# A graph layer on one core: three of five node blocks summed by weight matrices instead of two, blocks of 125 nodes

## The chip, the cores and the metric

One core of a Trainium2 chip. The metric is the device time of one execution in microseconds. The engines are named as in the profile: PE is TensorE, DVE is VectorE, ACT is ScalarE, POOL is GpSimd, SP is SyncE, which issues most DMAs.

## The reference

625 nodes with 512 features, 20,625 edges sorted by destination (20,000 random ones and one loop per node), four edge types with a weight matrix and a bias row each. Cut to what matters:

```python
h = relu(layernorm(x))
msg[e] = (h[src[e]] @ W_rel[type[e]] + b_rel[type[e]]) * weight[e]
agg = segment_sum(msg, dst) / maximum(segment_sum(weight, dst), 1)
z = h @ W_self + b_self + agg
x1 = layernorm(h + z) * ln1_g + ln1_b
ffn = gelu(x1 @ W_ffn1 + b_ffn1) @ W_ffn2 + b_ffn2
out = x + layernorm(x1 + ffn) * ln2_g + ln2_b
```

## The kernel before

Nodes lie in five blocks of 128 rows; 625 nodes leave a gap of 15 rows at the end of block 1. The work has two stages.

**The table stage.** For each relation r and block i, `table_rows` (L350) multiplies the transposed h of the block by W_rel[r] on PE (four matmuls of 512 columns into one PSUM bank). VectorE scales the rows by the norm's factor and adds b_rel, which lies in SBUF spread over all partitions (`brel_bc`), in one instruction (L362). SP stores the 128 rows to a table in DRAM (L365). The tiles m turn over three buffers; the last five of the 20 (`KEPT`) also stay in SBUF. Beside this loop, written out by hand in program order (L798 to L846), VectorE and GpSimd find for every node the window of 64 edge slots in which its edges lie (`find_tiles`, `find_windows`, gathers at L446), and edge indices become table rows (`edge_columns`).

**How an outer block is summed.** For the two blocks 0 and 4 (`dense`) the sum over edges is a matrix product: a weight matrix `sums_w` (table row by destination node, 20 chunks of 128 by 128) is multiplied by the whole table, 20 matmuls per block (`chunk_sum`, L1007). The weight matrix itself is built from the slots in four units per block. A unit is `slot_hots` on VectorE (five instructions: one-hot rows `low`, `eq`, three products `high`), then four banks of `slot_sums` on PE (L602), each emptied by a reduction on VectorE (L608). Before units begin, `turn_fields` transposes slot fields on PE. Five of the eight units are done in the table stage (`EARLY`), at most two banks behind a table row (`PER_ROW`). Table chunks that aren't kept are loaded two at a time (`chunk_load`, L1002, three buffers).

**How an inner block is summed.** For blocks 1 to 3, GpSimd gathers one table row per edge and partition, 128 edges to a gather (L887), after each fourth a pause of two small memsets (L883). Three gathers form a group, whose edges of one partition mostly share a destination: ScalarE scales the first (L893), VectorE adds the other two (L911), and PE multiplies the sum by a one-hot matrix of destinations (L930). Every second group is split into a high and a low part first (L897, L901), and then multiplied in two faster matmuls (L927, L928). There are 33 groups; rows whose group doesn't share a destination come in by six gathers of first rows (L937).

**The second stage** besides holds the self part (L375, L379), the first norm of each block, its transposition (L313, L1049), and the feed-forward part up (L685), Gelu (L689), down (L703), the second norm, the store (L754). Here the order on each engine comes from a planner (`Plan`, L69): each operation has an engine, an assumed duration, buffers, predecessors and a rank. It lists them in assumed time, and the resulting order is fixed in the program: an engine stops at an instruction whose input isn't there. The feed-forward parts follow the order 0, 4, 1, 2, 3 of blocks. If a check at run time finds edges outside the planned windows, a slow path at the end computes everything anew; it isn't taken here.

The loads are issued on SP in program order: x, W_rel of two relations, b_rel and the six bias and norm rows spread over 128 partitions early; others after each relation (`later_loads`, L227).

Of the kernel before, what the change touches and what calls it, by code (L numbers as in the profile page):

```python
# [16 lines left out]
P = 128  # L17
# [4 lines left out]
class EdgePlan:  # L22
# [3 lines left out]
    def __init__(self, n_nodes, n_tiles, n_free, nb):  # L26
# [15 lines left out]
        self.gap = nb * P - n_nodes  # L42
        self.gap_at = 2 * P - self.gap
        self.first = [b * P - (self.gap if b > 1 else 0) for b in range(nb)]
        self.size = [P - (self.gap if b == 1 else 0) for b in range(nb)]
# [19 lines left out]
    def row(self, node):  # L65
        return node + (self.gap if node >= self.gap_at else 0)
# [70 lines left out]
def gnn_layer(ctx, tc, x, edges, edge_groups, firsts, fourths, windows, w_self, w_rel, w_ffn1, w_ffn2, rows_in, bf1_in, out, n_edges):  # L137
# [22 lines left out]
    ep = EdgePlan(N, NT, n_edges - N, NB)  # L160
    NC = R * NB
# [24 lines left out]
    brel_bc = early.tile([P, R * D], F32, name="brel_bc")  # L186
# [7 lines left out]
    def load_x(b0, b1):  # L194
        nc.sync.dma_start(xs[:, b0:b1, :], x[ep.first[b0]:ep.first[b0] + (b1 - b0) * P, :].rearrange("(b p) d -> p b d", p=P))
# [24 lines left out]
    load_rows(brel_bc[:, :D], 0, D)  # L220
# [3 lines left out]
    load_rows(brel_bc[:, D:], D, R * D)  # L224
    load_rows(rows, R * D, (R + 6) * D)

    def later_loads(r):  # L227
        if r == 0:
            load_wr(2)
            nc.sync.dma_start(ws_sb, w_self.rearrange("(k p) n -> p k n", p=P))  # L230
            nc.sync.dma_start(bf1, bf1_in)
        if r == 1:
            load_wr(3)
            nc.sync.dma_start(w1_sb, w_ffn1.rearrange("(k p) f -> p k f", p=P))
        if r == 2:
            nc.sync.dma_start(w2_sb, w_ffn2.rearrange("(k p) n -> p k n", p=P))
# [17 lines left out]
    x_step = const.tile([P, INNER, EG], F32, name="x_step")  # L254
# [17 lines left out]
    grid = mid.tile([P, P, TB], BF16, name="grid")  # L272
    keys = mid.tile([P, 2 * NC, TP], BF16, name="keys")
    ident_b = mid.tile([P, P], BF16, name="ident_b")

    def node_constants():
# [11 lines left out]
        nc.gpsimd.iota(grid, pattern=[[1, P], [0, TB]], base=0, channel_multiplier=0,  # L288
                       allow_small_or_imprecise_dtypes=True)

    def aggregate(st, name, scaled=False):
        mv = work.tile([P, 2], F32, tag="mv", name=f"mv_{name}", bufs=HOTS)
        nc.vector.bn_aggr(mv, st)
        t = work.tile([P, 3], F32, tag="rs", name=f"rs_{name}", bufs=HOTS)
        if scaled:
            nc.vector.tensor_scalar(t[:, 0:1], mv[:, 1:2], EPS, RS ** -2, op0=ALU.add, op1=ALU.mult)
        else:
            nc.vector.tensor_scalar(t[:, 0:1], mv[:, 1:2], EPS, None, op0=ALU.add)
        return mv[:, 0:1], t
# [47 lines left out]
    KEPT = 5  # L347
    kept = {}

    def table_rows(r, i, between=None):  # L350
# [11 lines left out]
        nc.vector.scalar_tensor_tensor(m, p, rx[:, i, 1:2], brel_bc[:, r * D:(r + 1) * D],  # L362
                                       op0=ALU.mult, op1=ALU.add)
        row0 = r * NP + i * P
        nc.sync.dma_start(table[row0:row0 + P, :], m)  # L365
# [21 lines left out]
    node_of = early.tile([P, NT], I32, name="node_of")  # L387
# [14 lines left out]

    def edge_columns():
        nc.vector.tensor_copy(fl, ed[:, 0:3, :])
        nc.vector.tensor_scalar(shift, fl[:, 0:2, :], float(ep.gap_at), float(ep.gap), op0=ALU.is_ge, op1=ALU.mult)
        nc.vector.tensor_add(fl[:, 0:2, :], fl[:, 0:2, :], shift)
        nc.vector.scalar_tensor_tensor(row_i, typ_f, float(NP), src_f, op0=ALU.mult, op1=ALU.add)
        nc.vector.tensor_copy(node_of, dst_f)
        nc.vector.tensor_scalar(node_of, node_of, P - 1, None, op0=ALU.bitwise_and)
        nc.vector.tensor_copy(dst_mod, node_of)  # L410
# [60 lines left out]
    slots = early.tile([P, 3, ND, SL], I32, name="slots")  # L471
    fields = mid.tile([P, ND, 5, 2, SL], BF16, name="fields")
# [19 lines left out]
    def slot_fields():  # L492
        row, low, high = (slots[:, q] for q in range(3))
        src_, typ_, step, high_ = (slot_f[:, q] for q in range(4))
# [4 lines left out]
        nc.vector.tensor_scalar(step, src_, float(ep.gap_at), float(ep.gap), op0=ALU.is_ge, op1=ALU.mult)  # L499
        nc.vector.tensor_add(src_, src_, step)  # L500
        nc.vector.tensor_copy(row, src_)
        nc.vector.tensor_scalar(low, row, P - 1, None, op0=ALU.bitwise_and)
        nc.vector.tensor_scalar(high, row, 7, None, op0=ALU.logical_shift_right)
        nc.vector.tensor_copy(fields[:, :, 0], both(low))
        nc.vector.tensor_copy(high_, high)
        nc.vector.scalar_tensor_tensor(fields[:, :, 1, 0], typ_, float(NB), high_, op0=ALU.mult, op1=ALU.add)
# [6 lines left out]

    def first_edges():
        before_node(before[:, 2, :], ends_w[:, :, 0:4], 4)
        nc.vector.scalar_tensor_tensor(before[:, 2, :], at_f[:, 1, :], 4.0, before[:, 2, :], op0=ALU.mult, op1=ALU.add)
        near = 1.5 * 2.0 ** 23
        g = xw[:, 1, :]
        nc.vector.tensor_scalar(g, before[:, 2, ND:], -(GROUP0 * P + (EG - 1) / 2), 1.0 / EG, op0=ALU.add, op1=ALU.mult)
        nc.vector.tensor_scalar(g, g, near, None, op0=ALU.add)  # L520
        nc.vector.tensor_scalar(g, g, -near, 0.0, op0=ALU.add, op1=ALU.max)
# [8 lines left out]
    def first_columns():  # L530

        nc.vector.tensor_copy(x_cols, x_edges[:, :, :, 0:3])
        for f in range(2):
            nc.vector.tensor_scalar(x_step, x_cols[:, :, :, f], float(ep.gap_at), float(ep.gap), op0=ALU.is_ge, op1=ALU.mult)
            nc.vector.tensor_add(x_cols[:, :, :, f], x_cols[:, :, :, f], x_step)
# [38 lines left out]
    def slot_hots(d, u):  # L574
# [4 lines left out]
        low = mid.tile([P, nb_, P, TB], BF16, tag="low", name=f"low_{d}_{u}", bufs=2)  # L579
# [6 lines left out]
        nc.vector.tensor_tensor(low, of[:, 0].rearrange("p (a t) -> p a t", t=TB).unsqueeze(2).to_broadcast([P, nb_, P, TB]),  # L586
                                grid.unsqueeze(1).to_broadcast([P, nb_, P, TB]), op=ALU.is_equal)
# [6 lines left out]
    def slot_sums(d, u, q, low, high, place):  # L594
        if (d, u, q) == (d, 0, 0):
            sums_w[OUTER[d]] = const.tile([P, NC, P], F32, name=f"sums_w{d}")
# [3 lines left out]
        for i in range(QT):  # L600
            t = q * QT + i
            nc.tensor.matmul(p[:, i * W:(i + 1) * W], low[:, t // TB, :, t % TB], high[:, t // TP, :, t % TP],  # L602
# [3 lines left out]
    def empty_sums(d, u, q, p):  # L606
        n0 = 2 * (u * UNIT + q * QT)
        nc.vector.tensor_reduce(  # L608
            sums_w[OUTER[d]][:, :, n0:n0 + 2 * QT].rearrange("p c (t h) -> p t h c", h=2),
            p[:, :QT * 3 * 2 * NC].rearrange("p (t a h c) -> p t h c a", t=QT, a=3, h=2),  # L610
# [64 lines left out]
    def feed_forward(x1T_b, box, members, name, halves=False):  # L675
# [15 lines left out]
        def down(i):  # L691
# [14 lines left out]
            def summed(h):  # L706
                c = cols[h]
                if h == 0:
                    got["y"] = edge.tile([P, D], F32, tag="ow", name=f"y_{name}_{i}", bufs=OW)
                    got["st"] = work.tile([P, 2, 6], F32, tag="bn", name=f"st_y{name}_{i}", bufs=HOTS)  # L710
                    if n < P:
                        nc.vector.tensor_copy(got["y"], zi)
                nc.vector.tensor_add(got["y"][:n, c], po[h][:n, :c.stop - c.start], zi[:n, c])  # L713

            def stats_(h):
                nc.vector.bn_stats(got["st"][:, h, :], got["y"][:, cols[h]])

            def mean_():
                got["mean"], got["t"] = aggregate(got["st"][:, :len(cols), :], f"y{name}_{i}")

            def centred():
                got["a"] = edge.tile([P, D], F32, tag="ow", name=f"ya_{name}_{i}", bufs=OW)
                nc.vector.scalar_tensor_tensor(got["a"], got["y"], got["mean"], g2_bc,
                                               op0=ALU.subtract, op1=ALU.mult)

            def scaled():
                for c in (slice(0, 5 * D // 8), slice(5 * D // 8, D)) if halves else cols:
                    nc.vector.scalar_tensor_tensor(got["y"][:, c], got["a"][:, c], got["t"][:, 1:2], xi[:, c],
# [7 lines left out]
            for h in range(len(cols)):  # L736
                w = (cols[h].stop - cols[h].start) / D
                norm.append((f"y{h}", "DVE", 0.66 * w + (0.5 if n < P else 0.0), lambda h=h: summed(h),
# [37 lines left out]
    EARLY = 5  # L776
    PER_ROW = 2
    with tc.manual_schedule(engines={PE, DVE, ACT, mybir.EngineType.Pool}):
# [460 lines left out]
```

## Time and profile before

| What | us |
|---|---|
| Median of three runs (lowest, highest) | 285.38 (283.54, 285.41) |
| The profiled execution | 286.26 |
| Its span, first to last instruction | 284.5 |
| PE busy in the span | 248.5 |
| DVE busy | 198.4 |
| ACT busy | 51.5 |
| POOL busy | 139.9 |

The page's busy times are per engine; PEld, the load of weights into PE, overlaps PE. A float matmul appears as two records, so 80 products appear as x160. In a group of instructions the figures behind the bar are busy time, the mean of one in ns, and the idle time of the engine just before them with what ended it. In the timeline a matmul's start is when it begins to stream and its end is modelled, so durations of neighbours overlap; the distance of starts is the pace. In the table by stage, a count stands behind each busy time, then the TensorE clock that was granted (1.00 is full), the busy share of the DMA engines and the rate.

### The profile page before, as it was taken

Reading aid. Unit: us, or ns where it says so; the run is one execution under the profiler, and the core shown is the slowest. Engines: PE = TensorE matmul, PEld = TensorE weight load, DVE = VectorE, ACT = ScalarE, POOL = GpSimd, SP = SyncE. Lnnn points to the kernel's source line nnn. Section 1 sums busy time; section 2 is a strip of 40 time slices with the busy share of each in tenths; the row PEclk is TensorE's granted clock in tenths of the full one; section 3 lists DMA queues with packets and bytes.
Section 4 is the critical chain, followed back from the end, with each engine's and each line's share of the span. In section 5 each row is a group of like instructions: output and inputs, shape, how many; then the busy total and the mean of one; then the engine's idle time right before and its main releaser. Section 6 shows DMA issues by size and latency. Waiting matters only on the chain.

```text
span 284.5 us, 3070 instructions
## 1 busy us (share of the span) xinstructions
PE 248.5 (87%) x952; PEld 138.4 (49%) x952; DVE 198.4 (70%) x451; ACT 51.5 (18%) x104; POOL 139.9 (49%) x196
## 2 busy tenths in 40 slices
PE   7989949999999899999887999738999999744991
PEld 2534414555544454454345745316849576313970
DVE  5561777897697997967694499785567888494014
ACT  3100000000100020211022422202505342200330
POOL 6153610000500477777777777777777777711000
PEclk9999998999999999999998999975999999975797
DMA  7999992511112978898887666766656676721001
GB/s 248 333 415 393 382 352 106 184 74 74 42 50 97 318 210 295 253 317 312 292 325 234 185 187 215 209 199 183 189 154 186 183 208 192 217 75 38 0 2 39
DMA packets 22693, 56.69 MB, mean 199 GB/s; under 512 B 3057, under 2 KB 3777, under 8 KB 22546
## 3 DMA queue, kind: packets, MB, share of 16 engines
q0 software_dynamic: 8896, 28.29, 33.3%
q1 hardware_dynamic: 13632, 28.05, 27.2%
q8 instruction: 8, 0.13, 0.2%
q10 hardware_dynamic: 146, 0.13, 0.1%
q14 instruction: 11, 0.09, 0.1%
HBM read 49.93 MB, written 6.52 MB: 198 GB/s over the span
## 4 chain that ended last, share of the span: by engine, by line
PE 26%; DMA 21%; DVE 19%; POOL 16%; issue 13%; ACT 2%; SPq 1%; POOLq 0%; ACTq 0%; DVEq 0%
DMA ms<-table,row_i 15%; PE pt L355 10%; POOL ms L887 10%; PE pu L685 8%; PE po L703 4%; DVE ea L911 3%; DMA xs<-in_x_dram 3%; DMA win<-in_windows_dram,at_i 2%; PE acc L930 2%; POOL dst L446 2%; DVE es L911 2%; DVE sums_w L608 1%; POOL zeros L883 1%; DVE z L942 1%; ACT ea L893 1%
## 5 line engine op out<-in xcount | busy, mean ns | idle before, releaser
L887 POOL DMA_INDIRECT ms<-table,row_i x99 | 99.3, 1003 | 51.0 <-issue 24.2
L355 PE MATMUL pt<-wr,hT 128*128 128x512 f32 x160 | 73.6, 608 | 0.0
L685 PEld LDWEIGHTS pu<-x1T,w_sb 128*128 128x128 f32 x320 | 43.2, 216 | 7.7 <-issue 4.2
L911 DVE SCALAR_TENSOR_TENSOR ea<-ms,wgt_g,ea 128x512 f32<-128x512 f32 x43 | 32.3, 750 | 19.3 <-ACT ea L893 11.0
L355 PEld LDWEIGHTS pt<-wr,hT 128*128 128x128 f32 x160 | 29.8, 195 | 31.9 <-issue 31.0
L685 PE MATMUL pu<-x1T,w_sb 128*128 128x128 f32 (+1 forms) x320 | 43.4, 299 | 2.0 <-ACT x1T L1049 2.0
L893 ACT ACTIVATE ea<-ms,ed 128x512 f32<-128x512 f32 x33 | 22.8, 691 | 114.8 <-DMA ms<-table,row_i 70.8
L930 PE MATMUL acc<-es,oh 128*128 128x512 f32 x46 | 27.0, 671 | 14.8 <-DVE es L911 14.8
L703 PE MATMUL po<-w_sb,gT 128*128 128x512 f32 (+3 forms) x96 | 36.4, 522 | 0.0
L1007 PE MATMUL acc<-tr,sums_w 128*128 128x512 f32 x60 | 29.0, 598 | 0.0
L703 PEld LDWEIGHTS po<-w_sb,gT 128*128 128x128 f32 (+1 forms) x96 | 16.5, 188 | 14.0 <-issue 11.4
L911 DVE SCALAR_TENSOR_TENSOR es<-ms,wgt_g,ea 128x512 f32<-128x512 f32 x23 | 17.1, 744 | 8.0 <-DMA ms<-table,row_i 7.9
L362 DVE SCALAR_TENSOR_TENSOR m<-pt,rx,brel_bc 128x512 f32<-128x512 f32 x20 | 15.0, 748 | 10.0 <-PE pt L355 8.2
L526 POOL DMA_INDIRECT x_edges<-in_edge_groups_dram,x_group x3 | 2.8, 947 | 37.1 <-DVE x_group L522 36.5
L608 DVE TENSOR_REDUCE sums_w<-bank 128x160 f32<-128x480 f32 x32 | 20.0, 651 | 0.0
L930 PEld LDWEIGHTS acc<-es,oh 128*128 128x128 f32 x46 | 7.9, 200 | 24.3 <-DVE es L911 22.1
L375 PE MATMUL pz<-ws_sb,hT 128*128 128x512 f32 x40 | 18.6, 597 | 0.0
L602 PEld LDWEIGHTS <-low 128*128 128x128 bf16 x128 | 11.5, 147 | 13.2 <-issue 11.2
L689 ACT ACTIVATE gT<-pu,bf 128x128 f32<-128x128 f32 (+1 forms) x40 | 13.7, 362 | 21.1 <-PE pu L685 20.9
L1007 PEld LDWEIGHTS acc<-tr,sums_w 128*128 128x128 f32 x60 | 10.9, 190 | 9.8 <-issue 9.1
L713 DVE TENSOR_TENSOR y<-po,z 128x512 f32<-128x512 f32 (+3 forms) x6 | 3.6, 598 | 17.1 <-PE po L703 17.0
L883 POOL MEMSET zeros<- 128x200 bf16 x48 | 13.2, 274 | 1.4
(160 smaller groups left out, 235.9 us busy)
## 6 DMA issues: line engine op xcount, KB each, us to landing
tr<-table SPq DMA_DIRECT2D x14, 512.0 KB, 5.5
table<-m SPq DMA_DIRECT2D x20, 256.0 KB, 2.3
w_sb<-in_L_gnn_W_ffn_dram SPq DMA_DIRECT2D x2, 2048.0 KB, 10.8
wr<-in_L_gnn_W_rel_dram SPq DMA_DIRECT2D x3, 1024.0 KB, 9.0
ms<-table,row_i POOLq DMA_INDIRECT x99, 3.8
rows<-in_rows_dram SPq DMA_DIRECT2D x1, 1536.0 KB, 13.3
ws_sb<-in_L_gnn_W_self_dram SPq DMA_DIRECT2D x1, 1024.0 KB, 10.6
brel_bc<-in_rows_dram SPq DMA_DIRECT2D x1, 768.0 KB, 10.9
```

Source lines behind the costliest of these rows:

```text
L355: nc.tensor.matmul(p, hT[i][:, k, :], wr_sb[r][:, k, :], start=(k == 0), stop=(k == KD - 1))
L362: nc.vector.scalar_tensor_tensor(m, p, rx[:, i, 1:2], brel_bc[:, r * D:(r + 1) * D], op0=ALU.mult, op1=ALU.add)
L375: nc.tensor.matmul(p[0], hT[i][:, k, :], ws_sb[:, k, :], start=(k == 0), stop=(k == KD - 1))
L608: nc.vector.tensor_reduce(sums_w[OUTER[d]][:, :, n0:n0 + 2 * QT].rearrange("p c (t h) -> p t h c", h=2), p[:, :QT * 3 * 2 * NC].rearrange( ...
L685: nc.tensor.matmul(pu[:, :nn], w1_sb[:, k, f * P:(f + 1) * P], x1T_b()[:, k, :nn], start=(k == 0), stop=(k == KD - 1))
L703: nc.tensor.matmul(po[h][:n, :w], box["gT"][:, f, at], w2_sb[:, f, c], start=(f == 0), stop=(f == KF - 1))
L883: nc.gpsimd.memset(zeros[:, :PAUSE], 0.0)
L887: nc.gpsimd.indirect_dma_start(out=ms[j], out_offset=None, in_=table[:, :], in_offset=bass.IndirectOffsetOnAxis(ap=row_i[:, j:j + 1], axis=0))
L893: nc.scalar.activation(box["sum"], ms[j], AF.Copy, scale=wgt[:, j:j + 1])
L911: nc.vector.scalar_tensor_tensor(to, ms[j], wgt_g[:, k, q - 1:q], box["sum"], op0=ALU.mult, op1=ALU.add)
L930: nc.tensor.matmul(acc[bs], ohs[0][:, q, :].bitcast(F32), box["sum"], start=(k == 0), stop=last)
L1007: nc.tensor.matmul(acc[b,], sums_w[b][:, c, :], kept[(b, c) if (b, c) in kept else c], start=first, stop=last)
```

## The change

Blocks have 125 nodes each, in tiles of 128 rows (`NG = 125`). Blocks 0, 1, 2 are summed by weight matrices, blocks 3 and 4 by gathers. Row 125 of each chunk of the table holds b_rel of its relation, and row 125 of each weight matrix holds sums of the edge weights (a column of ones in `low`), so that b_rel comes in with the chunk sums. For the gathered blocks it comes in by one matmul of degrees by relation (`deg_T`) and b_rel. Table rows are evicted by ScalarE, 125 of them, without a bias, and stored from 125 partitions. `sums_w` has two buffers for three blocks: the units of block 2 come after the chunk sums of block 0. Seven of twelve units are early, at most three banks behind a table row; nine chunks are kept. Loads of bias rows, W_self and the feed-forward weights are issued later. The feed-forward order is 0, 1, 3, 2, 4. Some planner levels are changed. The core of the diff:

```diff
-        self.dense = (0, nb - 1)
+        self.dense = tuple(range(nb - 2))
...
+        self.each = -(-n_nodes // nb)
+        self.first = [b * self.each for b in range(nb)]
...
     def row(self, node):
-        return node + (self.gap if node >= self.gap_at else 0)
+        return node // self.each * P + node % self.each
...
-    load_rows(brel_bc[:, :D], 0, D)
...
-    load_rows(brel_bc[:, D:], D, R * D)
-    load_rows(rows, R * D, (R + 6) * D)
+    nc.sync.dma_start(brel, brel_in[:, :D])
...
         if r == 0:
             load_wr(2)
-            nc.sync.dma_start(ws_sb, w_self.rearrange("(k p) n -> p k n", p=P))
-            nc.sync.dma_start(bf1, bf1_in)
+            bias_rows()
         if r == 1:
             load_wr(3)
+            nc.sync.dma_start(ws_sb, w_self.rearrange("(k p) n -> p k n", p=P))
+            load_rows(rows, 0, 6 * D)
+            nc.sync.dma_start(bf1, bf1_in)
+        if r == 2:
             nc.sync.dma_start(w1_sb, w_ffn1.rearrange("(k p) f -> p k f", p=P))
-        if r == 2:
             nc.sync.dma_start(w2_sb, w_ffn2.rearrange("(k p) n -> p k n", p=P))
...
-    KEPT = 5
+    KEPT = 9
...
+    def bias_rows():
+        n = (P - NG) * D
+        nc.sync.dma_start(bass.AP(tensor=table.tensor, offset=table.offset + NG * D, ap=[[NP * D, R], [P * D, NB], [1, n]]),
+                          bass.AP(tensor=brel_in.tensor, offset=brel_in.offset, ap=[[n, R], [0, NB], [1, n]]))
...
             m = kept[c] = const.tile([P, D], F32, name=f"m_{c}")
+            nc.sync.dma_start(m[NG:NG + 1, :], brel_in[r:r + 1, :D])
...
-        nc.vector.scalar_tensor_tensor(m, p, rx[:, i, 1:2], brel_bc[:, r * D:(r + 1) * D],
-                                       op0=ALU.mult, op1=ALU.add)
+        nc.scalar.activation(m[:NG], p[:NG], AF.Copy, scale=rx[:NG, i, 1:2])
         row0 = r * NP + i * P
-        nc.sync.dma_start(table[row0:row0 + P, :], m)
+        nc.sync.dma_start(table[row0:row0 + NG, :], m[:NG])
...
+    def relation_degrees():
...
+        for r in range(R):
+            nc.vector.scalar_tensor_tensor(of[:, :, r, :], typ_, float(r), slot_w[:, ND:], op0=ALU.is_equal, op1=ALU.mult)
+        nc.vector.reduce_sum(deg, of, axis=mybir.AxisListType.X)
...
+            for n in range(INNER):
+                nc.tensor.transpose(p[:R, n * P:(n + 1) * P], deg[:, n, :], ident)
...
-            sums_w[OUTER[d]] = const.tile([P, NC, P], F32, name=f"sums_w{d}")
+            sums_w[OUTER[d]] = const.tile([P, NC, P], F32, tag="sums_w", name=f"sums_w{d}", bufs=2)
...
-    EARLY = 5
-    PER_ROW = 2
+    EARLY = 7
+    PER_ROW = 3
...
                     transposed(hT[i + 1], z[:, i + 1, :], f"h{i + 1}")
-                    next_norm(i + 2)
+                    next_norm(i + 2 if i == 0 else i + 3)
...
                     if i == 0:
+                        next_norm(3)
                         find_tiles()
...
-                if (r, i) >= (1, 2) and waiting and len(later) + len(sums_now) <= PER_ROW:
+                if (r, i) >= (1, 3) and waiting and len(later) + len(sums_now) <= UNIT // QT:
...
-    together = [[b] for b in ep.order]
+    together = [[b] for b in (*OUTER[:-1], *inner[:-1], OUTER[-1], inner[-1])]
...
+            if len(bs) == 1:
+                nc.tensor.matmul(acc[bs], deg_T[:, bs[0] - B0, :], brel, start=True, stop=False)
...
-        nc.sync.dma_start(t[:, :n, :], table[c * P:(c + n) * P, :].rearrange("(k p) d -> p k d", p=P))
+        nc.sync.dma_start(t[:NG + 1, :n, :], table[c * P:(c + n) * P, :].rearrange("(k p) d -> p k d", p=P)[:NG + 1])
...
+            free = m[OUTER[d - 2]] if d >= 2 and u == 0 else None
```

More of the change, by code (lines that the diff above doesn't have):

```diff
@@ L37, in __init__ @@
             window.append((lo, hi))
-        self.dense = (0, nb - 1)
+        self.dense = tuple(range(nb - 2))
         self.inner = [b for b in range(nb) if b not in self.dense]
         self.order = [*self.dense, *self.inner]
[L42 to L45, printed above, removed]
+        self.each = -(-n_nodes // nb)
+        assert self.each < P
+        self.first = [b * self.each for b in range(nb)]
+        self.size = [min(self.each, n_nodes - n) for n in self.first]
         b0, b1 = self.inner[0], self.inner[-1]
@@ L492, in slot_fields @@
     def slot_fields():
-        row, low, high = (slots[:, q] for q in range(3))
-        src_, typ_, step, high_ = (slot_f[:, q] for q in range(4))
+        src_, typ_, block, low = (slot_f[:, q] for q in range(4))
         rest = found[:, :ND, :SL]
@@ L843, in gnn_layer @@
             later_loads(r)
+        assert not waiting
         for d, u, q in sums_now + later:
@@ L995, in gnn_layer @@
             m = op("DVE", 0.72, lambda b=b, bs=bs, half_=half_: add_to(b, lambda: acc[bs], half_),
-                   after=[m], give=["acc"] if b == bs[-1] else [], rank=(0.3, n), level=0.45)
+                   after=[m, own[b]], give=["acc"] if b == bs[-1] else [], rank=(0.3, n), level=0.45)
             adds[b].append(m)
@@ L1006, in chunk_sum @@
             acc[b,] = ps_one.tile([P, D], F32, tag="one", name=f"acc{b}")
-        nc.tensor.matmul(acc[b,], sums_w[b][:, c, :], kept[(b, c) if (b, c) in kept else c], start=first, stop=last)
+        nc.tensor.matmul(acc[b,], sums_w[b][:NG + 1, c, :], kept[(b, c) if (b, c) in kept else c][:NG + 1],
+                         start=first, stop=last)
+    m, ld, t, here = {b: None for b in OUTER}, None, None, {}
     summed, h, e = {}, None, None
-    for i, (d, u) in enumerate(units[EARLY:]):
-        box = {}
-        h = op("DVE", 2.6, lambda d=d, u=u, box=box: box.update(hots=slot_hots(d, u)), after=[h], take=["low"],
-               rank=(0.55, i), level=0.4)
-        for q in range(UNIT // QT):
-            mm = op("PE", 0.28, lambda d=d, u=u, q=q, box=box: box.update(p=slot_sums(d, u, q, *box["hots"], (ps, "ps"))),
-                    after=[h, e], take=["ps"], give=["low"] if q == UNIT // QT - 1 else [], lag=0.25,
-                    rank=(2, 1 + 0.01 * i), level=0.55)
-            e = op("DVE", 0.56, lambda d=d, u=u, q=q, box=box: empty_sums(d, u, q, box["p"]), after=[mm], give=["ps"],
-                   rank=(0.5, i), level=0.4)
-        summed[d] = e
```

190 lines of the change are left out of this document (115 added, 75 removed).

## Prediction

> **What bounds the kernel now.** I read the page from the top (busy shares, slices), then busy time by stage, then TensorE's timeline and its waits, to see why a TensorE that is 87% busy is not the only bound.
>
> ```profile
> PE 248.5 (87%) x952; PEld 138.4 (49%) x952; DVE 198.4 (70%) x451; ACT 51.5 (18%) x104; POOL 139.9 (49%) x196
> PE   7989949999999899999887999738999999744991
> ```
>
> ```profile
> core 0: us, PE busy (x) PEld busy (x) DVE busy (x) ACT busy (x) POOL busy (x), PEclk, DMA share, GB/s
> 0.00:42.00 42.00, 34.78 (x98) 15.59 (x99) 23.95 (x79) 4.54 (x9) 16.80 (x27) 0.99 0.96 353
> 42.00:90.80 48.80, 48.65 (x183) 24.03 (x183) 40.64 (x88) 1.68 (x4) 3.59 (x15) 0.97 0.26 97
> 90.80:180.00 89.20, 83.77 (x289) 43.26 (x288) 71.10 (x147) 19.32 (x34) 65.05 (x83) 0.98 0.79 255
> 180.00:200.00 20.00, 12.49 (x43) 7.65 (x42) 13.29 (x29) 3.70 (x7) 15.27 (x21) 0.74 0.68 198
> 200.00:240.00 40.00, 40.00 (x225) 28.68 (x224) 30.44 (x68) 14.09 (x34) 30.69 (x40) 1.00 0.65 186
> 240.00:261.00 21.00, 11.82 (x26) 4.47 (x24) 14.96 (x34) 3.38 (x6) 8.46 (x11) 0.81 0.42 128
> 261.00:284.50 23.50, 17.00 (x96) 14.69 (x96) 4.06 (x12) 4.79 (x12) 0.00 (x0) 0.79 0.04 13
> ```
>
> Until 90.8 the table of messages is made and TensorE is the bound. After that GpSimd gathers rows, and TensorE does everything else beside it. Between 200 and 240 us it is busy for 40.00 of 40 us at full clock although the gathers still run: it had feed-forward work ready. In 180 to 200 and 240 to 261 it had none: 12.49 of 20 and 11.82 of 21 us, and the clock granted fell with it. So the gathers set the end only where nothing else is left for TensorE.
>
> ```profile
> 95.10 1.06 POOL L887 DMA_INDIRECT ms<-table,row_i  x1 [18.14 <-DMA table<-m]
> 248.72 0.95 POOL ms L887
> PE acc L930 <- DVE es L911: 14.8, 9, 3.2
> 261.21 10.05 PE pu L685 x64
> 271.26 6.96 PE po L703 x32
> ```
>
> (The first and last gather from GpSimd's timeline and the chain, a wait of TensorE, the last two steps of the chain on TensorE.) 99 gathers of edge rows and 6 of first rows take 95.1 to 249.7 us, 154.6/105 = 1.47 us each. The last block then follows alone: its norm, 64 matmul passes up at a low clock, 32 down, done at 278.2, and 6.3 us of norm and store.
>
> **The sum: TensorE's own work.** Four passes of the timeline give its pace (a new group starts when the one before has been streamed).
>
> ```profile
> 50.79 3.65 PE L355 MATMUL pt<-wr,hT 128*128 128x512 f32 x8
> 54.28 0.66 PE L602 MATMUL bank<-high,low 128*128 128x120 bf16 x8
> 54.78 3.65 PE L355 MATMUL pt<-wr,hT 128*128 128x512 f32 x8
> 125.80 0.48 PE L927 MATMUL acc<-eh,oh 128*128 128x512 f32 x1
> 126.35 1.02 PE L1007 MATMUL acc<-tr,sums_w 128*128 128x512 f32 x2
> 169.85 3.60 PE L1007 MATMUL acc<-tr,sums_w 128*128 128x512 f32 x8
> 173.28 0.60 PE L313 MATMUL tp_x<-ident,x 128*128 128x128 f32 x4
> 173.72 1.88 PE L1007 MATMUL acc<-tr,sums_w 128*128 128x512 f32 x4
> 203.85 1.02 PE L930 MATMUL acc<-es,oh 128*128 128x512 f32 x2
> 204.71 1.05 PE L685 MATMUL pu<-x1T,w_sb 128*128 128x128 f32 x8
> 205.60 3.60 PE L703 MATMUL po<-w_sb,gT 128*128 128x512 f32 x8
> 209.04 1.02 PE L930 MATMUL acc<-es,oh 128*128 128x512 f32 x2
> ```
>
> A float matmul of 512 columns (two records) takes 0.86 us: 3.43/4 in a table chunk, 0.86 in an edge sum, 3.44/4 in the feed-forward. A table row (four) takes 3.49 with its weights, one bank of slot sums 0.50/2 = 0.25, a split edge sum 0.55, the transposes of a block 0.44, the upward part of a block 64 x 0.89/8 = 7.1 and the downward 8 x 0.86 = 6.9, so 14.0.
>
> From 90.8 on TensorE has, before: self part 20 x 0.86 = 17.2; 12 banks 3.0; 40 chunk sums 34.4; 33 groups of three gathers, of which 23 plain 19.8 and 10 split 5.5; five blocks of feed-forward 70.0; transposes 2.2. Sum 152.1, against 278.2 - 90.8 = 187.4 elapsed: 35.3 lost to idle time and low clock.
>
> After: the planner's arithmetic gives 23 groups (11 for block 3, 2 shared, 10 for block 4), 8 of them split. So 17.2; 20 banks 5.0 (seven of twelve units are done early, five are left); 60 chunk sums 51.6; 15 plain 12.9; 8 split 4.4; two matmuls that add b_rel by degree 1.7 (contracting over 4 rows, but 512 columns as elsewhere); 70.0; 2.2. Sum 165.0: 12.9 us **more**. (17.2 + 2.0 + 1.7 for the dense block and the degrees, less 6.9 + 1.1 for ten groups.)
>
> **The table stage, part by part.** TensorE has two waits there, which the new order meets (rows of TensorE's timeline, then of the chain and VectorE's timeline).
>
> ```profile
> 16.66 0.66 PE L313 MATMUL tp_h<-ident,z 128*128 128x128 f32 x4 [1.36 <-DVE rx L330]
> 39.75 0.23 PE L569 MATMUL tf<-ident_b,fields 128*128 128x128 bf16 x1 [3.12 <-DVE fields L504]
> 41.84 8.62 PE L355 MATMUL pt<-wr,hT 128*128 128x512 f32 x16
> 67.19 1.13 DVE sums_w L608 x2
> 68.32 1.13 DVE low L586
> 69.45 0.41 DVE eq L588
> 69.89 1.30 DVE high L591 x3
> 38.54 0.29 DVE L500 TENSOR_TENSOR slot_f<-slot_f 128x128 f32<-128x128 f32 x1
> ```
>
> The norm of block 3 moves ahead of the tile search on VectorE: -1.4. The turning of the fields moves from behind row (1,2) to behind (1,3): TensorE had no table row from 39.75 - 3.12 = 36.6 to 41.8, and one row of 3.5 us fills that: -3.5. The fields of three blocks instead of two and other index arithmetic: chain about 1 us longer, but 2.5 MB of broadcast b_rel and bias rows leave the first 42 us, where the DMA share is 0.96, so I take it as even (between +1 and -3). Two more slot units early: 8 banks, +2.0; degree transposes +0.2. That is 88.1.
>
> VectorE is the doubt. It loses the 11 evictions in this stretch (0.75 each, row below, 8.2) and gains two units of 1.13 + 0.41 + 1.30 + 4 x 0.57 = 5.1 each, and the degrees by relation (a cast, four products of the size of L500's 0.29, a sum over 512 at the 0.57 of a bank), 2.2 with the starts. 40.6 - 8.2 + 10.2 + 2.2 = 44.8 of 48 us; TensorE stands behind slot sums that VectorE has not prepared. I put 2.4 us there (between 0 and 5): the table is done at 90.5, against 90.8.
>
> ```profile
> L362 DVE SCALAR_TENSOR_TENSOR m<-pt,rx,brel_bc 128x512 f32<-128x512 f32 x20 | 15.0, 748 | 10.0 <-PE pt L355 8.2
> L893 ACT ACTIVATE ea<-ms,ed 128x512 f32<-128x512 f32 x33 | 22.8, 691 | 114.8 <-DMA ms<-table,row_i 70.8
> table<-m SPq DMA_DIRECT2D x20, 256.0 KB, 2.3
> tr<-table SPq DMA_DIRECT2D x14, 512.0 KB, 5.5
> rows<-in_rows_dram SPq DMA_DIRECT2D x1, 1536.0 KB, 13.3
> ```
>
> (Two groups of the page, then DMA issues with their time to landing.) ScalarE's eviction is not in the trace. The nearest row, a product by a column on the same engine, is 0.691 us, VectorE's own 0.748; ScalarE is busy for 6.2 of the first 90.8 us, so 20 x 0.69 = 13.8 hides, and its queue holds only the hT copies. Between -0.06 and +0.1 us at the last row, taken as 0. If ScalarE were held, TensorE would stop after four PSUM banks.
>
> Stores of 125 rows and chunk loads of 126 are not in the trace either. The whole-tile store lands in 2.3 us; no less is to be expected from 2% fewer bytes, and a bound above is the 5.5 us of a store's double. Three m tiles turn over in 3 x 3.5 = 10.5 us, so even 5.5 plus an eviction holds no row; the last one would delay the gathers by up to 3.2 us, which is off TensorE's path. I take 2.3 to 3.6, at no cost. [...]
>
> The moved loads: ws_sb and rows are issued after the second relation (about 46 us) and first read in the fourth (about 72 us); 26 us hold a transfer of 13.3 and the megabytes beside it, as the DMA share there is 0.26. w1 and w2 follow at about 68, read after 120. Late, they would hold VectorE's ws_sb and g rows, and the evictions no longer stand behind these. Nine one-row loads and the copy of the bias rows join SyncE's queue ahead of stores that have 10.5 us: nothing, unless they hold that queue for more than this.
>
> **The second stage.** GpSimd: 69 + 4 = 73 gathers x 1.47 = 107.5 us from about 95: done at 202 instead of 250. If the rest followed as before (284.5 - 249.7 = 34.8) the end would be 237: gathers no longer set it; TensorE at 90.5 + 165.0 does. VectorE: the stage loses 20 row additions (0.75), two splits and some small ones, about 19, and gains two units, 10: it ends less loaded over the whole, but its slot units fall in the first half, where it is 71.1 of 89.2 us busy. What is lost on TensorE: from 90.8 to 180.7 it did 81.0 us of work by these paces in 89.9: a tenth, while VectorE and gathers feed it. For the 108 us of gathers that is 11; after 202, as in 200 to 240, nothing, and the last block's upward part needs 7.1 instead of 10.05 since block 2's feed-forward stands before it.
>
> Span: 90.5 + 165.0 + 11 + 6.3 = 272.8. The profiled execution took 286.26 for a span of 284.5, so 1.8 is added: 274.6, say **275 us**. That execution is 0.3% above the median of 285.38; the comparison is with 286.
>
> **Rivals.**
> - *TensorE waits as much as now.* Its order is fixed; an edge sum waiting for VectorE (14.8 us in 9 waits) stops ready matmuls behind it, and VectorE now builds five slot units beside the row additions. For it: 80% of VectorE in 90.8 to 180 before the units are added. Against: 40.00 of 40 in 200 to 240 with edge sums in between. With a loss of 35.3: 90.5 + 165 + 35.3 + 6.3 + 1.8 = 299. It decides from a loss of 23 us on.
> - *The third weight matrix comes late.* Only two sums_w exist, so block 2's units start after block 0's 20 chunk sums. From a start T: four units of 5.1 with their banks (22), 17.2 of sums, a norm of seven steps of 0.75, two feed-forwards 28, 6.3: T + 79. I expect T near 125; from 200 on it takes back all the gain: about 281 to 288.
> - *Almost no loss.* Fewer gathers, less DMA, more ready work: loss under 6, 265 to 270. Against it stands the tenth lost where the same mix ran.
>
> **How the numbers follow.** Forecast, loss 6 to 18: 270 to 282, chance 0.55. Almost no loss: 0.12. Late matrix, 282 to 288: 0.11. TensorE waits on, above 288: 0.22. One per cent, 2.9 us, is about what can be told from no change: faster below 282.5 0.67, same 0.11, slower 0.22. The range 266 to 291 leaves out a little of the second case (0.03) and most of the last (0.17). Given only the likeliest case it would be 270 to 282.
>
> **What would show it.** Right: L362 on ScalarE at some 0.7 us and hidden; the last table row near 90; 73 gathers ending near 202; TensorE without gaps from there to about 266; upward part of the last block in 7 us. Wrong: idle TensorE behind edge sums or behind block 2's slot sums; a table done after 95; gathers waiting for VectorE.

## The result and the profile after

The changed kernel takes 302.97 us (median of four runs, 301.71 to 304.07), the kernel before 285.39 beside it (283.54 to 287.73): a ratio of 1.061, interval 1.052 to 1.070. It is 6% slower. The profiled execution took 304.07 us with a span of 302.2. The forecast was 275, the range ended at 291. A few executions fall in a slower state (four of the ten of e1_w128 below); the medians hold all runs, the ratios and their intervals only the others.

The page of the changed kernel, busy shares and slices:

```profile
PE 283.5 (94%) x1047; PEld 174.3 (58%) x1047; DVE 188.5 (62%) x440; ACT 60.1 (20%) x115; POOL 102.3 (34%) x146
PE   7999949999999999999697979999999999999991
PEclk9999987999999999999999979999999999999997
```

TensorE is busy for 35.0 us more than before, where 15.1 us more of work were forecast (12.9 after the table, 2.2 in its stage). The gaps near the end are gone, as forecast, and so is the low clock there (granted 0.81 and 0.79 after 240 us before, now 1.00 from 200 to 295.4). TensorE isn't waiting more; it is doing something that takes longer than was thought. Busy time by stage of the changed kernel (columns as in the table before) says where:

```profile
0.00:42.00 42.00, 37.51 (x101) 16.74 (x101) 17.91 (x63) 10.72 (x18) 16.60 (x29) 1.00 0.70 242
42.00:90.80 48.80, 47.55 (x150) 30.79 (x149) 37.18 (x88) 7.54 (x13) 2.48 (x9) 0.93 0.45 157
90.80:110.00 19.20, 19.20 (x70) 13.81 (x69) 10.03 (x20) 2.06 (x3) 0.00 (x0) 1.00 0.16 49
110.00:180.00 70.00, 63.79 (x184) 34.87 (x182) 50.03 (x99) 12.26 (x20) 48.58 (x62) 0.98 0.86 247
200.00:240.00 40.00, 40.00 (x174) 25.32 (x173) 34.25 (x85) 12.26 (x25) 21.11 (x29) 1.00 0.51 143
261.00:295.40 34.40, 34.40 (x194) 24.86 (x193) 11.56 (x33) 7.93 (x19) 0.00 (x0) 1.00 0.05 16
```

The table stage now lasts to 110 instead of 90.8, with TensorE busy, GpSimd idle and ScalarE nearly so (2.06 of 19.2 us). In 42 to 90.8 TensorE gets through 150 matmul records instead of 183, and its weight loads (PEld) are busy for 30.8 us instead of 24.0. The timeline of TensorE in that stage, one table row and one set of slot sums after the other:

```profile
88.83 2.75 PE L631 MATMUL bank<-high,low 128*126 128x120 bf16 x12
91.42 3.65 PE L366 MATMUL pt<-wr,hT 128*128 128x512 f32 x8
94.91 2.75 PE L631 MATMUL bank<-high,low 128*126 128x120 bf16 x12
97.50 3.65 PE L366 MATMUL pt<-wr,hT 128*128 128x512 f32 x8
```

A table row takes 94.91 - 91.42 = 3.49 us as before. Three banks take 91.42 - 88.83 = 2.59, 0.86 each, where they took 0.25. The groups by form name the difference. First the kernel before, then the changed one (x is 128 and 192 weight loads):

```profile
L602 PEld LDWEIGHTS <-low 128*128 128x128 bf16 x128 | 11.5, 147 | 13.2 <-issue 11.2 <-DVE high L591 1.0 <-DVE sums_w L608 0.5
```

```profile
L631 PEld LDWEIGHTS <-low 128*126 128x126 bf16 x192 | 48.5, 321 | 9.9 <-issue 6.4 <-DVE low L614 0.2 <-DVE x_step L419 0.2
L732 PEld LDWEIGHTS po<-w_sb,gT 128*125 128x125 f32 x96 | 16.5, 188 | 15.2 <-issue 13.0
L714 PEld LDWEIGHTS pu<-x1T,w_sb 128*128 128x128 f32 x320 | 36.9, 192 | 1.4 <-issue 1.4
```

A bf16 weight of 126 columns loads in 321 ns, one of 128 columns in 147. Float weights don't show it: 125 columns 188, 128 columns 192. The cut to 125 nodes and one row for b_rel had made the one-hot weights `low` 126 columns wide. 48 banks by 0.61 us are 29.5 us. That is the theory which the experiments below test; the rival is that TensorE has waits in this stage anyway, so that the banks only fill them and the loss comes from elsewhere.

### The profile page after: what moved, and what is told of

Its sections match the earlier page's. It is cut to its first block, busy times and chain, and to the rows that moved or that the text cites. A ratio compares the mean times of both kernels' runs of the same rounds, so it can differ in the third digit from the quotient of the medians.

```text
span 302.2 us, 3190 instructions
## 1 busy us (share of the span) xinstructions
PE 283.5 (94%) x1047; PEld 174.3 (58%) x1047; DVE 188.5 (62%) x440; ACT 60.1 (20%) x115; POOL 102.3 (34%) x146
## 3 DMA queue, kind: packets, MB, share of 16 engines
q0 software_dynamic: 6304, 19.89, 23.2%
## 4 chain that ended last, share of the span: by engine, by line
PE 73%; DMA 12%; DVE 6%; issue 4%; POOL 3%; SPq 1%; DVEq 0%; POOLq 0%
PE acc L1043 14%; PE pt L366 14%; PE bank L631 12%; PE pu L714 12%; PE po L732 11%; PE pz L386 5%; DMA tr<-table 4%; DMA ms<-table,row_i 4%; PE acc L966 3%; DMA xs<-in_x_dram 2%; DMA win<-in_windows_dram,at_i 2%; POOL dst L462 2%; PE acc L960 1%; POOL win L462 1%; PE acc L964 1%
## 5 line engine op out<-in xcount | busy, mean ns | idle before, releaser
L919 POOL DMA_INDIRECT ms<-table,row_i x69 | 69.0, 1000 | 70.6 <-DVE eq L617 33.7
L631 PEld LDWEIGHTS <-low 128*126 128x126 bf16 x192 | 48.5, 321 | 9.9 <-issue 6.4
L637 DVE TENSOR_REDUCE sums_w<-bank 126x160 f32<-126x480 f32 x48 | 31.2, 656 | 30.7 <-PE bank L631 30.7
L631 PE MATMUL bank<-high,low 128*126 128x120 bf16 x192 | 44.3, 367 | 0.0
L714 PE MATMUL pu<-x1T,w_sb 128*128 128x125 f32 x320 | 37.8, 276 | 0.0
L1043 PE MATMUL acc<-tr,sums_w 126*128 126x512 f32 x66 | 32.7, 626 | 3.7 <-DMA tr<-table 3.7
L732 PE MATMUL po<-w_sb,gT 128*125 128x512 f32 (+2 forms) x96 | 35.7, 521 | 0.0
L732 PEld LDWEIGHTS po<-w_sb,gT 128*125 128x125 f32 x96 | 16.5, 188 | 15.2 <-issue 13.0
L1043 PE MATMUL acc<-m,sums_w 126*128 126x512 f32 x54 | 25.2, 596 | 0.0
L1043 PEld LDWEIGHTS acc<-tr,sums_w 126*128 126x128 f32 x66 | 12.4, 199 | 16.3 <-issue 11.6
L620 DVE TENSOR_TENSOR high<-eq,turned 128x640 bf16<-128x640 bf16 x36 | 15.5, 487 | 0.4
```

Of the source, the lines that this page charges most:

```text
L620: nc.vector.tensor_mul(high[:, :, a * 2 * NC:(a + 1) * 2 * NC, :], eq, pairs(2 + a))
L631: nc.tensor.matmul(p[:NG + 1, i * W:(i + 1) * W], low[:, t // TB, :, t % TB], high[:, t // TP, :, t % TP], start=True, stop=True)
L637: nc.vector.tensor_reduce(sums_w[OUTER[d]][:NG + 1, :, n0:n0 + 2 * QT].rearrange("p c (t h) -> p t h c", h=2), p[:NG + 1, :QT * 3 * 2 * NC ...
L714: nc.tensor.matmul(pu[:, :nn], w1_sb[:, k, f * P:(f + 1) * P], x1T_b()[:, k, :nn], start=(k == 0), stop=(k == KD - 1))
L732: nc.tensor.matmul(po[h][:n, :w], box["gT"][:, f, at], w2_sb[:, f, c], start=(f == 0), stop=(f == KF - 1))
L919: nc.gpsimd.indirect_dma_start(out=ms[j], out_offset=None, in_=table[:, :], in_offset=bass.IndirectOffsetOnAxis(ap=row_i[:, j:j + 1], axis=0))
```

## Experiments

Each was compared with the kernel before on the same chip; r is the ratio to it with its interval. Steps between kernels are differences of r times 285.4 us. The edits are shown by their main lines.

**The width of the weights.** The tile gets 128 columns, of which two are not read afterwards:

```diff
-    lows = [mid.tile([P, SL // 4 // TB, NG + 1, TB], BF16, name=f"low_{n}") for n in range(2)]
+    lows = [mid.tile([P, SL // 4 // TB, P, TB], BF16, name=f"low_{n}") for n in range(2)]
...
-            nc.tensor.matmul(p[:NG + 1, i * W:(i + 1) * W], low[:, t // TB, :, t % TB], high[:, t // TP, :, t % TP],
+            nc.tensor.matmul(p[:, i * W:(i + 1) * W], low[:, t // TB, :, t % TB], high[:, t // TP, :, t % TP],
```

> The changed kernel with the one-hot tile low widened from 126 to 128 columns, so that the slot sums load 128 columns of weights instead of 126 (the extra columns hold ones and their sums aren't read). Theory, width: a bank cost 2.59/3 = 0.86 us with 126 columns and 0.25 with 128 before the change; 48 banks give back 48 x 0.61 = 29.5 us, all of it on TensorE's path: weight loads near 146 ns instead of 327, table done near 90, time near 273 (270 to 278). Rival, waits: the banks only fill time in which TensorE would wait anyway for VectorE or for the third weight matrix; then TensorE shows new gaps and the time stays at 285 or above.

284.53 us (280.54 to 286.25, ten runs), r = 0.990 (0.985 to 0.996): 20 us less than the change as it was. The weight loads of this kernel:

```profile
L631 PEld LDWEIGHTS <-low 128*128 128x128 bf16 x192 | 16.9, 147 | 15.3 <-issue 14.6 <-DVE high L620 0.5 <-DVE eq L617 0.2
```

The mechanism is right, the size is not: the theory said 273, and a third of the 29.5 us is not won. With TensorE quicker something else came to wait, which is taken up below.

The same tile, of which 126 columns are loaded, tells the width from the address of the half tiles:

```diff
-            nc.tensor.matmul(p[:NG + 1, i * W:(i + 1) * W], low[:, t // TB, :, t % TB], high[:, t // TP, :, t % TP],
+            nc.tensor.matmul(p[:NG + 1, i * W:(i + 1) * W], low[:, t // TB, :NG + 1, t % TB], high[:, t // TP, :, t % TP],
```

> The changed kernel with the tile low of 128 columns, of which the slot sums still load 126. Theory, width: nothing changes, weight loads near 327 ns, time near 303. Rival, address: the half tiles now start 2048 bytes apart instead of 2016, and if that was the cause the loads fall to about 146 ns and the time to about 273.

300.89 us, r = 1.049 (1.040 to 1.059), weight loads 321 ns. It is the width.

And the other side, the kernel before with 126 columns (its reductions and chunk sums then use 126 rows too):

```diff
-            nc.tensor.matmul(p[:, i * W:(i + 1) * W], low[:, t // TB, :, t % TB], high[:, t // TP, :, t % TP],
+            nc.tensor.matmul(p[:126, i * W:(i + 1) * W], low[:, t // TB, :126, t % TB], high[:, t // TP, :, t % TP],
```

> The kernel before with the slot sums' weights cut to 126 columns (what the last two table rows of each chunk add to the two outer blocks is left out). Theory, width: 32 banks cost 0.61 more each, 19.5 us; the 20 banks of the table stage, 12.2 us, are all on TensorE's path, the other 12 partly hidden beside the gathers: 297 to 305. Rival, the cause lies elsewhere in the change: 285, loads at 146 ns.

298.43 us, r = 1.043 (1.038 to 1.048), weight loads 320 ns: the one detail alone makes the old kernel 4% slower, as forecast.

**The chunk loads.** In the chain of waits of the changed kernel stands a chunk load of 12.7 us, in that of e1_w128 one of 10.5 (start, duration from the issue). In the kernel before, where whole tiles are loaded, 14 of the 16 loads have a time to landing, 6.1 us at most and most of them beside gathers (third fence: least, median and most).

```profile
163.21 12.68 DMA tr<-table
```

```profile
148.99 10.51 DMA tr<-table
```

```profile
DMA to landing us min/median/max: 3.3/5.3/6.1
```

They move 126 rows instead of 128. Rows 126 and 127 of the table hold zeros, so whole tiles can be loaded:

```diff
-        nc.sync.dma_start(t[:NG + 1, :n, :], table[c * P:(c + n) * P, :].rearrange("(k p) d -> p k d", p=P)[:NG + 1])
+        nc.sync.dma_start(t[:, :n, :], table[c * P:(c + n) * P, :].rearrange("(k p) d -> p k d", p=P))
```

> As e1_w128, and the table chunks are loaded in 128 rows instead of 126. In the changed kernel TensorE waited 3.7 us for these loads, at a DMA share near 1 and 280 GB/s, where before 0.92 went with 329. Theory, the number of rows decides over how many DMA engines a load runs: the DMA share falls and the waits go, 1 to 4 us below e1_w128. Rival: no difference, within 1 us.

275.34 us, r = 0.964 (0.959 to 0.969), 7.5 us below e1_w128, more than expected. In e1_w128 the chunk sums on TensorE wait for loads (us in total, times, longest); in e4_load128 none of them does.

```profile
PE acc L1043 <- DMA tr<-table: 2.9, 2, 1.7
```

The semaphore updates in the kept traces give each load's time from issue to landing, which includes queueing behind other loads in flight (in the changed kernel three issued at 110.19, 110.58 and 111.05 land after 4.1, 5.5 and 7.1 us): 3.6 to 7.4 us in e4_load128 (median 5.7 of 18 loads), 3.9 to 10.5 in e1_w128 (median 7.7). The 7.5 us are more than TensorE's direct wait of 2.9; what carries the rest was not followed.

Five variants of the same load came next, on the base of e1_w128 or e4_load128, to learn what makes it slow. Three of the theories count DMA engines by the number of rows. The traces show how many are busy where transfers of one shape are alone under way: a store of 128 rows (kernel before), one of 125 and loads of 126 (changed kernel), columns as in the tables by stage:

```profile
60.20:60.60 0.40, 0.40 (x3) 0.16 (x2) 0.40 (x2) 0.00 (x0) 0.00 (x0) 1.00 1.05 410
```

```profile
98.00:98.80 0.80, 0.80 (x3) 0.37 (x2) 0.80 (x2) 0.00 (x0) 0.00 (x0) 1.00 0.32 115
246.90:247.30 0.40, 0.40 (x3) 0.16 (x2) 0.36 (x1) 0.00 (x0) 0.00 (x0) 1.00 0.92 358
```

Of 16 engines 0.32 is 5, and 0.92 to the whole tile's 1.05 is 14. In these two traces the semaphore of a transfer is updated 16 times for 128 and for 112 rows, 15 times for 126 and 6 times for 125.

```diff
+        for p0, p1 in ((0, 112), (112, NG + 1)):
+            nc.sync.dma_start(t[p0:p1, :n, :], table[c * P:(c + n) * P, :].rearrange("(k p) d -> p k d", p=P)[p0:p1])
```

> As e1_w128 (284.5 us), with each chunk load of 126 rows cut into one of 112 and one of 14 rows. The same bytes and rows are moved. Theory, the number of rows sets how many engines a load runs on: 112 rows run on 16, and the time falls to that of 128 rows, 275 to 277. Rival, the last two rows themselves or their place in memory matter: stays near 284.

282.25 us, r = 0.990 (0.982 to 0.997). Not the 275 that the count of engines would give.

```diff
+        nc.sync.dma_start(t[:NG, :n, :], table[c * P:(c + n) * P, :].rearrange("(k p) d -> p k d", p=P)[:NG])
```

> As e1_w128, with chunk loads of 125 rows (b_rel of the loaded chunks is left out). Theory, a row count that shares a smaller factor with 16 or less engines runs on fewer: 126 = 14 x 9, 125 = 5 x 25; a load slows from about 10 us to 15 or more, the chunk sums wait for it, 295 to 330. Rival, any row count other than a multiple of 16 costs the same: near 284.

303.19 us (two runs), r = 1.059 (1.052 to 1.067). So row counts do differ: 125 is far worse than 126. (Chunk sums of loaded chunks use 125 rows here.)

```diff
+        for p0, p1 in ((0, 120), (120, NG + 1)):
```

> As e1_w128 (284.5 us), with each chunk load cut into 120 and 6 rows. 112 and 14 gave 282.3, with loads still 9 us long, so the count of engines alone does not explain the cost of 126 rows. Theory, rows to an engine: in 128 rows each engine has 8, in 112 seven, in 126 nine; with 120 rows as 15 engines of 8 the load is as good as whole: 275 to 278. Rival, only the whole 128 rows are spread well: 280 to 285.

285.57 us, r = 0.999 (0.992 to 1.006): this theory fell. That 120 rows run on 15 engines was the author's estimate and is not shown.

```diff
+        for p0, p1 in ((0, 64), (64, P)):
```

> As e4_load128 (275.3 us), with each chunk load of 128 rows cut into two of 64. A control for the number of DMAs. Theory, twice as many DMAs cost nothing, since their shape decides: 275 to 277. Rival, what kept 112 and 14 rows slow was the second DMA: 280 to 284.

285.43 us, r = 0.999 (0.991 to 1.007). The control failed: two DMAs of 64 rows are no faster than 126 rows. That left the number of DMAs against their row count.

```diff
+        for k in range(n):
+            nc.sync.dma_start(t[:, k, :], table[(c + k) * P:(c + k + 1) * P, :])
```

> As e4_load128 (275.3 us), with each chunk load cut by chunk instead of by row: two DMAs of 128 rows of 2 KB. Twice the DMAs, all rows whole. Theory, the shape decides (a transfer over fewer than 128 rows is slow): 274 to 277. Rival, the second DMA as such was the cost of 64 and 64 rows: 280 to 286.

276.05 us, r = 0.969 (0.962 to 0.976): twice the DMAs of whole 128 rows cost nothing measurable. So here the number of DMAs doesn't decide, but whether each has all 128 rows. Loads in the chains of waits of e6_load112_14, e7_load125 and e10_load64_64, in this order:

```profile
150.60 9.40 DMA tr<-table
```

```profile
129.56 17.70 DMA tr<-table
```

```profile
142.58 10.92 DMA tr<-table
```

And TensorE's waits for loads in e6_load112_14, e7_load125, e9_load120_6 and e10_load64_64; e13_load_by_chunk, like e4_load128, has none:

```profile
PE acc L1044 <- DMA tr<-table: 3.2, 4, 1.1
PE acc L1044 <- DMA tr<-table: 14.8, 5, 5.1
PE acc L1044 <- DMA tr<-table: 4.6, 4, 2.9
PE acc L1044 <- DMA tr<-table: 2.8, 1, 2.8
```

And the kernel before with 126 rows (chunk sums over 126 rows for loaded chunks):

```diff
-        nc.sync.dma_start(t[:, :n, :], table[c * P:(c + n) * P, :].rearrange("(k p) d -> p k d", p=P))
+        nc.sync.dma_start(t[:126, :n, :], table[c * P:(c + n) * P, :].rearrange("(k p) d -> p k d", p=P)[:126])
```

> The kernel before (285.5 us) with chunk loads of 126 rows (the last two rows of the loaded chunks are left out of the sums). Theory, the loads slow from 5.5 to some 10 us there too, but its gathers set the end and only one of the two dense blocks is summed where the DMA engines are full: 286 to 291. Rival, no difference: 285.

287.49 us, r = 1.005 (0.999 to 1.012): no difference that the interval shows. There the gathers set the end; that the slower loads (up to 9.6 us in its kept trace) are off the path fits this, and was not tested further.

**The table stores.** On the base of e4_load128, 125 rows cut in two:

```diff
-        nc.sync.dma_start(table[row0:row0 + NG, :], m[:NG])
+        for p0, p1 in ((0, 112), (112, NG)):
+            nc.sync.dma_start(table[row0 + p0:row0 + p1, :], m[p0:p1])
```

> As e4_load128, with each table store of 125 rows cut into one of 112 and one of 13 rows. In the changed kernel 5.7 us lie between the issue of the last store and the first gather, 3.3 before. Theory: stores land sooner, the wait of an eviction for its buffer (4.8 us at 36) goes and the gathers start 2 us earlier, but neither is on TensorE's path: 274 to 276, as e4_load128. Rival, the start of the gathers sets the time: 2 to 3 us faster.

268.89 us, r = 0.941 (0.935 to 0.946), 6.7 us below e4_load128. The theory that an edit of the stores leaves the time alone was wrong. Two places show where the time went. First the row in which the wait for the edge windows ends on VectorE, in e4_load128 and then e8_store112_13:

```profile
38.14 0.35 DVE L493 CAST ends<-win 128x192 f32<-128x192 int32 x1 [6.49 <-DMA win<-in_windows_dram,at_i]
```

```profile
35.06 0.35 DVE L494 CAST ends<-win 128x192 f32<-128x192 int32 x1 [3.33 <-DMA win<-in_windows_dram,at_i]
```

With 125 rows to a store VectorE has the windows, gathered by GpSimd, 3 us later; everything up to the slot units hangs on them, and the table is done at 91.5 instead of 88.4. That the shape of the stores slows these gathers is not shown, since beside the whole-tile stores of e14_store128 below they are no quicker. Their median time to landing in e4_load128, e8_store112_13 and e14_store128:

```profile
win<-in_windows_dram,at_i POOLq DMA_INDIRECT x5, 6.1
win<-in_windows_dram,at_i POOLq DMA_INDIRECT x5, 4.2
win<-in_windows_dram,at_i POOLq DMA_INDIRECT x5, 6.3
```

A rival is the order of SyncE's queue: in e8_store112_13 the 1.5 MB of bias and norm rows are issued at 33.9 us instead of 23.2, and from 25 to 30 us the DMA engines are 0.52 busy instead of 0.97. No run holds that order fixed. Second, the first gather, in the same order (GpSimd's timeline), and then two evictions on ScalarE at the same row of the table:

```profile
97.58 0.95 POOL L919 DMA_INDIRECT ms<-table,row_i  x1 [25.37 <-DMA tr<-table]
41.23 0.69 ACT L374 ACTIVATE m<-pt,rx 125x512 f32<-125x512 f32 x1 [4.71 <-DMA table<-m]
```

```profile
91.33 1.08 POOL L920 DMA_INDIRECT ms<-table,row_i  x1 [22.25 <-issue]
39.21 0.69 ACT L374 ACTIVATE m<-pt,rx 125x512 f32<-125x512 f32 x1 [2.75 <-PE pt L366]
```

97.58 is 6.1 us after TensorE leaves the table at 91.5; 91.33 is 3.0 after 88.4. (The profile puts the first wait down to a chunk load, which was issued in between; a gather reads the table, so it is the stores that it needs.) The ring of three m tiles did hold an eviction for 4.7 us, and doesn't any more.

Whole stores, with b_rel loaded into each m first:

```diff
+        nc.sync.dma_start(m[NG:, :], brel_in[r, :].rearrange("(p d) -> p d", d=D))
...
-        nc.sync.dma_start(table[row0:row0 + NG, :], m[:NG])
+        nc.sync.dma_start(table[row0:row0 + P, :], m)
```

> As e4_load128, with table stores of whole tiles: b_rel and two rows of zeros are loaded into rows 125 to 127 of each m by a small DMA, and 128 rows are stored. Theory, the shape decides for stores too: gathers start about 3 us after the last store as with 112 and 13 rows (268.9 us), 267 to 271. Rival, twenty small loads in SyncE's queue and in the ring of three tiles cost what the shape brings: 272 to 278.

270.77 us, r = 0.952 (0.944 to 0.959): between 125 rows and 112 and 13; its interval touches both. Its first gather starts at 92.86, 2.9 us after TensorE leaves the table at 89.96, as with 112 and 13 rows, so what whole and cut stores share is this second place.

**Both DMA edits without the width.**

> The changed kernel (303 us) with 126-column weights as they are, but chunk loads of 128 rows and stores cut into 112 and 13 rows. With 128-column weights these two moved 284.5 to 268.9. Theory, the banks of slot sums (29.5 us of TensorE) are on the path whatever the DMAs do: 268.9 + 29.5 = 298, so between 294 and 300; TensorE is busier and hides part of what the loads cost. Rival, the DMAs were the larger part: 285 to 290.

291.94 us, r = 1.021 (1.015 to 1.028), between the two forecasts. From here the width alone brings 1.021 - 0.941, 22.8 us; the two DMA edits alone bring 1.061 - 1.021, 11.4 us from the change as it was. Together 34.2.

**Eviction by VectorE**, on the base of e4_load128:

```diff
-        nc.scalar.activation(m[:NG], p[:NG], AF.Copy, scale=rx[:NG, i, 1:2])
+        nc.vector.tensor_scalar(m[:NG], p[:NG], rx[:NG, i, 1:2], None, op0=ALU.mult)
```

> As e4_load128 (275.3 us), with the table rows evicted by VectorE again (one scaling instruction, no bias) instead of ScalarE. Theory: VectorE was busy for 43.6 of 48 us between 42 and 90 us in e4_load128; 11 evictions of some 0.67 are 7.4 more, so it becomes the bound there and TensorE's slot sums and table rows wait: table done 3 to 8 us later, time 278 to 284. Rival: VectorE's gaps take it, 275 to 276.

285.04 us, r = 0.994 (0.989 to 0.999), 8.6 us slower. Busy time of 42 to 90 us, e4_load128 and then e5_evict_dve:

```profile
42.00:90.00 48.00, 46.68 (x196) 24.02 (x196) 43.59 (x102) 8.93 (x15) 2.47 (x9) 0.96 0.50 174
```

```profile
42.00:90.00 48.00, 40.75 (x168) 20.92 (x169) 45.57 (x108) 2.04 (x5) 2.47 (x9) 0.93 0.48 166
```

VectorE is busy for 45.6 of 48 us and TensorE gets through 168 records instead of 196. ScalarE's eviction is what leaves VectorE room for the two more early units.

e8_store112_13 beats both kernels, with three blocks summed by weight matrices, 125 nodes to a block and eviction by ScalarE: the change as designed, with three tile shapes mended. Its page:

```profile
span 266.8 us, 3219 instructions
PE 252.4 (95%) x1047; PEld 141.5 (53%) x1047; DVE 185.9 (70%) x440; ACT 60.0 (22%) x115; POOL 103.1 (39%) x146
```

## Why the prediction was wrong

The span was forecast as 90.5 + 165.0 + 11 + 6.3 = 272.8. It was 302.2, and the 29.4 us between are accounted for by TensorE's timeline.

- **A bank of slot sums at 0.25 us: this step failed.** "20 banks 5.0", and eight more banks at 2.0 in the table stage, were priced from a row with 128 columns of bf16 weights, though the full diff of the kernels has 126. 28 banks in the table stage took 0.61 more each, 17.1 us, the 20 later ones 12.2. Together they are the size of the whole miss; the other errors, below, nearly cancel. A weight load was counted as hidden in the pace, and the pace was carried over to another width.
- **The table done at 90.5:** it was done at 109.95, 19.4 later. Beside the 17.1, the fields, taken as even "between +1 and -3", came 2.4 late: TensorE went on at 44.2, not 41.8. The first two table rows after that wait took 9.51 instead of 8.45 us, at a granted clock of 0.50 up to 49.4 us: 1.1 more. The -1.4 for block 3's norm was counted wrongly, since TensorE then waits for the fields anyway. Against these stand the 2.4 put down for VectorE's stalls: the timeline of TensorE shows none there once the rows run. Nor did the bias and norm rows leave the first 42 us: the load of 1.5 MB, expected at about 46, was issued at 23.1.

```profile
44.24 9.68 PE L366 MATMUL pt<-wr,hT 128*128 128x512 f32 x16
23.09 0.40 SPq L210 DMA_DIRECT2D rows<-in_rows_dram  x1
```

- **Loss of 11 us beside the gathers:** from 109.95 to TensorE's end at 295.4 there are 185.5 us, less 165.0 and 12.2, a loss of 8.3. In e4_load128 (table done at 91.5, TensorE's end at 267.0) it is 10.5. But for the banks, TensorE's own work was counted right.
- **Stores of 125 rows and loads of 126 "at no cost":** wrong, though hidden in the changed kernel's miss. Once TensorE was quick the edits of stores and loads brought 6.7 and 7.5 us. The bound of 5.5 us for a store's landing was too low: by the last update of their semaphores the changed kernel's stores took 3.8 to 11.5 us (median 5.2; whole tiles before 2.0 to 12.1, median 2.3), an eviction did wait for its tile, and the slowest chunk loads took 10.5 to 12.7. The 5 engines that 125 rows kept busy fit the slowest load in a chain of waits, 17.7 us in e7_load125. The count of engines doesn't cover the rest: the semaphore is updated 16 times for 112 rows, as for 128, and loads of 112 and 14 rows were as slow as 126 (r = 0.990 both); 64 and 64 gave 0.999.
- **Gathers done at 202, no longer the bound:** in e4_load128 the last starts at 206.8 and in e8_store112_13 at 199.9. Right. In the changed kernel they start at 112.7, after the late table, and end with 60 us of TensorE's work still to come.
- **Last block's upward part at 7.1:** 281.28 to 288.42, 7.1. Right, and the clock there is 1.00.
- **ScalarE's eviction hidden at 0.69:** 0.687 and hidden. Right; e5_evict_dve puts its worth at 8.6 us; the prediction had taken 8.2 us off VectorE's load for it, without a price in time of its own.

The rival "TensorE waits as much as now" named 299, near the result, for the wrong reason: TensorE waits less than before and is busy for 94%. A number that fits isn't a cause.

What stays open is why only whole tiles of 128 rows load fast. The number of DMAs is excluded (e13_load_by_chunk), the count of engines alone too (e6_load112_14). No run shows the part of a single engine in a load, so the cause is not shown. For the stores it is open how much of the 6.7 us is their shape and how much the order of the other loads.

## What to carry to other kernels

A shape that changes by two columns is a new operation: the price of a weight load, a store or a load must come from a row of the same shape, or be bounded as unknown. Here 126 columns instead of 128 cost 20 to 23 us, and the loads of 126 and stores of 125 rows some 14 more. Pad tiles to 128 in bf16 weights and in transfers, and keep the odd count for the data alone.

## What the runs showed of the hardware

- bf16 weights of 126 columns load in 321 ns (changed kernel), of 128 in 147 (kernel before, e1_w128); a matmul of 120 columns behind them runs at a pace of 216 instead of 62 ns. For float weights 125 and 128 columns are alike (188 and 192 ns, changed kernel).
- A load of about 0.5 MB, up to three in flight beside gathers, from issue to landing by the semaphore updates of the kept traces, median and longest: 128 rows 5.8 and 7.4 us (e4_load128); 126 rows 8.1 and 10.5 (e1_w128); 112 and 14 rows 7.7 and 11.2; 120 and 6 rows 8.2 and 12.6; 64 and 64 rows 8.1 and 11.6; 125 rows 15.1 and 23.5.
- Busy share of the 16 DMA engines, transfers of one shape alone under way: a store of 128 rows 1.05 by the profile, at 410 GB/s (kernel before), loads of 126 rows 0.92 at 358, a store of 125 rows 0.32 at 115 (changed kernel).
- Gathers that read a table start 6.1 us after the last row's matmuls where it is stored in 125 rows (e4_load128), and 2.9 to 3.0 us after where in 128 or in 112 and 13.
